# Splitting a softmax shift by batches, clearing key buffers early, and checking by a product, in a chain of four quantised transformer blocks

## The chip, the cores and the metric

The kernel runs on one core of a Trainium2 chip. The metric is the device time of one execution in microseconds (us), from the chip; lower is better. Each kernel was executed several times, and the median is quoted.

## The reference

The input x has 4 batches of 1024 tokens with 288 channels; a context of 64 tokens per batch and a mask (all zero here) come with it. Four blocks are applied one after the other, with 16 heads of 18 channels:

- Block 0: layer norm, self attention, layer norm, attention to the context, layer norm, and a feed-forward part of width 1152. All linear layers are quantised: each token's input is scaled by its largest absolute value and rounded to 8-bit levels, and the weights to levels per output channel.
- Block 1: attention to the context with two sets of keys and values ("vip"), added up.
- Block 2: self attention, context attention and a gated feed-forward part with *fake quantisation*: queries, keys, values and the probabilities of the softmax are rounded to levels of a step that belongs to the whole tensor. So the maximum over all probabilities of all batches has to be known before the first of them can be rounded.
- Block 3: as block 0, with other weights.

The cut of the reference that matters for the change is that of block 2's probabilities:

```python
def _fake_quant(x, n_bits, always_zero=False):
    levels = float(2 ** n_bits - 1)
    if always_zero:
        delta = jax.lax.stop_gradient(jnp.max(x) / levels)
        zp = jnp.float32(0.0)
```

## The kernel before

x stays in SBUF for the whole program as 32 tiles of 128 tokens (NT = 32, NTB = 8 tiles per batch). TensorE (PE) does the matmuls and the transposes, ScalarE (ACT) exponentials and copies, VectorE (DVE) reductions and rounding, GpSimd (POOL) residual additions and the affine part of the layer norms, and SyncE (SP) issues most DMAs. The framework's scheduler orders the instructions of one engine among each other; every engine then runs its own instructions strictly in that order, and a DMA queue runs in order too.

**Block 0 and block 1.** `quant_self` does the self attention of block 0. The stage after it (context attention, feed-forward, and block 1) is made of generators, such as `tokens(b, hf)` in `ctx_stage`, which do a piece of work and then yield a figure of what the next piece costs ("d8.5": 8.5 us of DVE; "a", "g" and "x" stand for other engines and waits). A planner, `run_stages`, plays these figures through and so decides in which order the pieces are emitted. The matmuls of context and vip keys (L2510, L2554), the transposes of quantised levels (L1349, copied out at L1354) and the quantised matmuls (L277) are such pieces. The statistics of a batch's layer norm come from `norm_stats`.

**Block 2, two passes.** `fq_passes` runs the self attention twice over the keys. Pass 1 (L2906, L2913) computes every score block, its exponential with the sum over keys (`sums`), and the largest exponential of each row (`top`), for 32 tiles of 16 heads: both are 128 x 512 arrays. From them `prob_shift` computes the largest probability of all, which needs a maximum over the partitions (`prob_params` calls GpSimd's partition_all_reduce, L826), and from it the step of the probabilities and, for each row, the number that has to be added to its scores so that the exponential comes out in units of that step. The shift needs a logarithm and an exponential (`log_shift`, L835 to L843; each function needs its own table in ScalarE), and it is cut into three bfloat16 parts (L2383, L2385) that add up to full precision. `watch_range` (L1218 to L1224) checks that reciprocals lie in a range.

`add_shift` (L2393 to L2400) then puts the three parts of one tile into spare channels of the queries: GpSimd copies them into a padded tile `spad`, TensorE transposes it (L2399), and VectorE adds it to the queries `qk` (L2400). The keys have ones in these channels. Pass 2 (`attend_levels`: scores L3299, exponential L3308, rounding L3311, product with the values L3282) works with key buffers `kz` in which the heads of a group are spread out; there are two, cleared once (L3006), and `spread` fills one by four DMAs (L3014). After pass 1, the order of the code is: `prob_shift` whole; loads of four parameters (L107, L113); the clearing of `spad` and `kz`; `spread(0)`; `add_shift` for the first tiles; then pass 2 with the other tiles' shifts between its score blocks.

The context attention of block 2 (`fq_tail`) calls `prob_shift` in the same way for its own probabilities. The loads of the feed-forward weights (L2408, L113), of biases (L3132) and of the first queries (L3142) follow it in SP's queue.

**The verdict.** The kernel assumes things of its data (ranges, zero points). Each assumption that is tested writes into a column of `self.bad`. At the end `verdict` takes the maximum over columns and partitions (all-reduce, L1202), reads it as an integer into the engines' registers, and a branch runs a general version of the program if it isn't zero. The last residual additions (L1747) and output DMAs (L2309) stand around it.

Of the kernel before, what the change touches and what calls it, by code (L numbers as in the profile page):

```python
# [18 lines left out]

# [2 lines left out]

# [29 lines left out]
EXP, GELU, SIDE = "exp", "gelu", "side"  # L52
# [3 lines left out]
class Net:  # L56
# [772 lines left out]

    def log_shift(self, pool, nm, sums, d, name):  # L830

        nc = self.nc
        n = sums.shape[1]
        y = pool.tile([P, n], F32, name=f"{name}y")
        nc.vector.tensor_scalar(y, sums, d, None, ALU.mult)  # L835
        z = pool.tile([P, n], F32, name=f"{name}z")
        nc.scalar.activation(z, y, AF.Ln)
        nc.vector.tensor_tensor(nm, nm, z, ALU.subtract)

        nc.scalar.activation(z, z, AF.Exp, scale=-1.0)  # L840
# [338 lines left out]
class Fast(Net):  # L1179
# [6 lines left out]
    def __init__(self, ctx, tc):  # L1186
        super().__init__(ctx, tc)
        self.bad = self.cp.tile([P, 96], F32, name="bad")
        self.n_bad = 0
        self.nmagic = self.cp.tile([P, 1], F32, name="nmagic")  # L1190
        self.nc.vector.memset(self.nmagic, -MAGIC)
        self.tiny = self.cp.tile([P, 1], F32, name="tiny")
        self.nc.vector.memset(self.tiny, 1e-8)
        self.nc.vector.memset(self.bad, 0.0)

    def verdict(self):

        nc = self.nc
        s = self.cp.tile([P, 1], F32, name="bads")
        nc.vector.tensor_reduce(s, self.bad, AX.X, ALU.max)  # L1200
        al = self.cp.tile([P, 1], F32, name="bada")
        nc.gpsimd.partition_all_reduce(al, s, P, bass_isa.ReduceOp.max)  # L1202
        fl = self.cp.tile([1, 1], mybir.dt.int32, name="badi")
        nc.vector.tensor_copy(fl, al[0:1, :])
        return nc.values_load(fl[0:1, 0:1])

    @contextmanager
# [556 lines left out]
    def quant_self(self, L, w, beside, ready):  # L1764
# [4 lines left out]
        tc, nc = self.tc, self.nc  # L1769
        with ExitStack() as es:  # L1770
# [30 lines left out]
            ep = pool(f"{L}ep", 6)  # L1801
# [5 lines left out]
            def levels(b):  # L1807

                hT = at.tile([CK, NC3, S], BF16, tag="hT", name="hT")
                srep = at.tile([P, S], F32, tag="srep", name="srep")  # L1810
                scs = []
                state[b] = {"hT": hT, "srep": srep, "sc": scs}
                stats = self.norm_stats(b, 1e-6)
# [163 lines left out]
            for b in range(B):  # L1977
                state[b]["a"] = at.tile([P, NTB, C], F32, tag="a", name="a")
                for g in range(NG):
                    if g + 1 < NG:  # L1980
                        side.insert(0, operands(b, g + 1))
                    elif b + 1 < B:
                        while side:
                            step()
                        side.append(operands(b + 1, 0))
                    if g == 1 and b + 1 < B:
                        side.append(levels(b + 1))
                        side.append(values(b + 1))
# [143 lines left out]
    def ctx_stage(self, cw, g2, b2, pool, nb):  # L2132
# [15 lines left out]
        def tokens(b, hf):  # L2148
            t0 = b * NTB + hf * 4
            if hf == 0:  # L2150
                stats[b] = self.norm_stats(b, 1e-5)
                there[b] = yield "d8.5", None, SIDE
            while b not in there:
                yield "x1", None, SIDE
            h = self.wk.tile([P, 4, C], F32, tag="h", name="h", bufs=nb)
# [209 lines left out]
    def prob_shift(self, gp, tp, top, sums, step):  # L2365


        nc = self.nc
        flat = lambda ap: ap.rearrange("p t h -> p (t h)")
        rstep = gp.tile([P, 1], F32, name="rstep")  # L2370
        nc.vector.reciprocal(rstep, step)
        r = tp.tile([P, NT * H], F32, name="rs")
        nc.vector.reciprocal(r, flat(sums))
        self.watch_range(self.R_MIN, self.R_MAX, r, "wr")
        u = flat(top)
        nc.vector.tensor_tensor(r, r, u, ALU.mult)
        pd = self.prob_params(gp, r, "pd")
        nc.vector.memset(u, 0.0)
        self.log_shift(tp, u, flat(sums), pd, "ls")
        nc.vector.tensor_scalar(u, u, rstep, None, ALU.mult)  # L2380
        parts = gp.tile([P, 3, NT * H], BF16, name="parts")
        for k in range(3):
            nc.vector.tensor_copy(parts[:, k, :], u)  # L2383
            if k < 2:
                nc.vector.tensor_tensor(u, u, parts[:, k, :], ALU.subtract)  # L2385
        return pd, parts

    def add_shift(self, qT, sp, parts, t):


        nc = self.nc
        for k in range(3):
            nc.gpsimd.tensor_copy(  # L2393
                sp[:, :, D + k : D + k + 1], parts[:, k, t * H : (t + 1) * H].unsqueeze(2)
            )
# [4 lines left out]
        nc.vector.tensor_tensor(  # L2400
            qT, qT, ps[:, : NG * P].rearrange("p (g t) -> p g t", t=P), ALU.add
        )
# [425 lines left out]
    def fq_passes(self, w, q, step, raw, rawq, qmx, qmn, side, aside):  # L2828

        tc, nc = self.tc, self.nc  # L2830
        with ExitStack() as es:
# [6 lines left out]
            v = gp.tile([P, NT, C + HP - D], BF16, name="v")  # L2838
            nc.gpsimd.memset(v[:, :, C:], 0.0)

            tops = ExitStack()
            tp = tops.enter_context(tc.tile_pool(name="f1m", bufs=1))
            top = tp.tile([P, NT, H], F32, name="top")
            sums = tp.tile([P, NT, H], F32, name="sums")
            with (
# [43 lines left out]
                for b in range(B):  # L2889
# [23 lines left out]
                                nc.vector.tensor_reduce(top[:, t, h0 : h0 + 2], e, AX.X, ALU.max)  # L2913
                    if ahead:
                        operands(b + 1, NTB - 1)
            with tops:
                pd, parts = self.prob_shift(gp, tp, top, sums, step)
            es.enter_context(self.psum("f1o"))

            pv = gp.tile([P, 1], F32, name="pv")  # L2920
            nc.vector.tensor_tensor(pv, pd, q["d"][:, 2:3], ALU.mult)
            nc.vector.tensor_scalar(wo, wo, pv, None, ALU.mult)
            at, ot, ep = pool("f1o", 1), pool("f1q", 2), pool("f1p", 2)
            g2 = self.load_bc(at, w["ln2_g"], C, "g2")
            b2 = self.load_bc(at, w["ln2_b"], C, "b2")
            bo2 = self.load_bc(at, w["bo2"], C, "bo2")
            wq2 = self.load_w(at, w["Wq2"], C, "wq2")
            spad = at.tile([P, H, HP], BF16, name="spad")
            nc.gpsimd.memset(spad, 0.0)

            def shifts(b, hf):
                for j in range(hf * 4, hf * 4 + 4):
                    t = b * NTB + j
                    self.add_shift(qk[:, b, 0, :, j * P : (j + 1) * P], spad, parts, t)
                    yield

            def output(t0, oT):

# [62 lines left out]
                        nc.sync.dma_start(rawq[t // NTB][:, t % NTB, :], y)  # L3001
                        yield

            kzs = [at.tile([P, 2, S], BF16, name=f"kz{n}") for n in range(2)]
            for kz in kzs:
                nc.gpsimd.memset(kz, 0.0)  # L3006

            def spread(n):

                kz = kzs[n % 2]  # L3010
                b, g = n // (2 * NG), n % NG
                for i in range(4):
                    rows = slice(i * HP, (i + 1) * HP)
                    nc.sync.dma_start(kz[rows, i % 2, :], qk[rows, b, 1, g, :])  # L3014

            spread(0)
            side.append(shifts(0, 0))
            while side:
                aside()
            late = []  # L3020
            for b in range(B):
                for qh in range(2):
                    side[:0] = [shifts(*divmod(2 * b + qh + 1, 2))] if 2 * b + qh + 1 < 2 * B else []
# [17 lines left out]
    def fq_tail(self, w, kq, keep, rawq, mx, nmn, beside):  # L3041
# [5 lines left out]
        with ExitStack() as es:  # L3047
# [6 lines left out]
            with (  # L3054
# [23 lines left out]
                for t in range(NT):  # L3078
# [35 lines left out]
                    e4 = self.wk.tile([P, H, T // 4], F32, tag="e4", name="e4")  # L3114
                    nc.gpsimd.tensor_tensor(e4, e2[:, :, : T // 4], e2[:, :, T // 4 :], ALU.add)
                    nc.vector.tensor_reduce(sums[:, t, :], e4, AX.X, ALU.add)
                pd, parts = self.prob_shift(gp, qp, top, sums, step)
            pv = gp.tile([P, 1], F32, name="pv")
            nc.vector.tensor_tensor(pv, pd, kq["d"][:, 1:2], ALU.mult)
            nc.vector.tensor_scalar(wo, wo, pv, None, ALU.mult)  # L3120
# [121 lines left out]
                before = t0  # L3242
            for _ in spare:
                pass
            self.weave([forward(before)], 1, 1)

    def scale_register(self, name, t):
# [176 lines left out]
```

## Time and profile before

| | |
|---|---|
| median of 3 runs | 5156.69 us (5151.0 to 5164.89) |
| the profiled execution | 5151.01 us, span 5149.3 us, mean granted TensorE clock 0.837 |
| busy share of the span | PE 85%, PE weight loads 34%, DVE 57%, ACT 61%, POOL 27% |
| instructions | 63938 |
| block 0 self attention | 0 to about 890 us |
| block 0 context, feed-forward, block 1 | 890 to 1664 us |
| block 2: layer norm, projections | 1664 to 1850 us |
| pass 1; gap; pass 2 | 1850 to 2437; to 2467; to 3023 us |
| queries, context pass, second gap | 3023 to 3200 us |
| probabilities and feed-forward | 3200 to 3846 us |
| block 3 | 3846 to 5149 us |

A profile is one execution with a record of each instruction: its engine, line, operands, start and duration. "Idle before" is the time in which the engine had nothing running before the instruction, followed by what ended it; "issue" means that no recorded event explains it. Lines are those of the kernel before, unless the kernel after is meant.

### The profile page before, as it was taken

The numbers are of one execution on the slowest core, as the hardware profiler recorded it, in microseconds if no ns is written. First come the engines' busy times: TensorE is split into PE (matmuls) and PEld (weight loads), VectorE is DVE, ScalarE is ACT, GpSimd is POOL, SyncE is SP. The second block draws the span as 40 slices with busy tenths as digits, with TensorE's granted clock in tenths as the row PEclk, the third lists the DMA queues.
The fourth block names the chain that finished last, engine by engine and source line by source line (L and its number), as shares of the span: only waits on it lengthen the run. The fifth ranks groups of instructions, "written<-read, shape, count | busy, mean of one in ns | idle before, by whom it ended". The sixth has DMA issues, their size and how long they took to land. (4 is left out here: it accounts for less than half of the span.)

```text
span 5149.3 us, 63938 instructions
## 1 busy us (share of the span) xinstructions
PE 4374.8 (85%) x23291; PEld 1746.7 (34%) x23291; DVE 2952.4 (57%) x6478; ACT 3130.4 (61%) x4422; POOL 1394.7 (27%) x2173
## 2 busy tenths in 40 slices
PE   5999998788898979998688864899988999996786
PEld 2223222445566421100233332454542223222343
DVE  8333244665554579999688777332334334334775
ACT  3766666466653259998888853222215666674796
POOL 4020111542321566200222234111113111103664
PEclk8999998889999965555788775899997999997897
DMA  2000001200001221000000032000000000001000
GB/s 75 4 5 12 3 21 46 75 27 14 3 12 38 110 84 38 11 1 0 23 26 24 24 98 77 21 15 10 1 15 1 8 4 9 18 21 31 16 17 20
DMA packets 135639, 136.01 MB, mean 26 GB/s; under 512 B 69260, under 2 KB 111884, under 8 KB 133648
## 3 DMA queue, kind: packets, MB, share of 16 engines
q1 hardware_dynamic: 134112, 128.13, 8.3%
q0 software_dynamic: 1200, 3.69, 0.3%
q8 instruction: 185, 3.03, 0.2%
q14 instruction: 142, 1.16, 0.1%
HBM read 79.92 MB, written 43.47 MB: 24 GB/s over the span
## 5 line engine op out<-in xcount | busy, mean ns | idle before, releaser
L2004 ACT ACTIVATE e<-ps 128x1024 f32<-128x1024 f32 x1024 | 998.6, 1021 | 483.1 <-PE ps L1994 473.0
L1994 PE MATMUL ps<-qT,kT 32*128 32x512 f32 x4096 | 704.1, 662 | 4.4 <-ACT e L2004 4.4
L1954 PE MATMUL ps<-e,v 128*32 128x512 f32 x4096 | 575.7, 627 | 10.2 <-DVE oT L1965 7.7
L2913 DVE TENSOR_REDUCE top<-e 128x2 f32<-128x2048 f32 x256 | 561.9, 2275 | 18.5 <-ACT e L2906 18.5
L2906 ACT ACTIVATE e<-ps 128x1024 f32<-128x1024 f32 x512 | 534.1, 1369 | 19.6 <-PE ps L3259 11.3
L3308 ACT ACTIVATE e<-ps 128x1024 f32<-128x1024 f32 x512 | 483.9, 1059 | 88.0 <-PE ps L3299 70.5
L3259 PE MATMUL ps<-qk 32*128 32x512 bf16 x1024 | 511.1, 604 | 24.3 <-ACT e L2906 23.0
L1747 POOL TENSOR_TENSOR x<-x,y 128x288 f32<-128x288 f32 x192 | 151.9, 802 | 826.4 <-DVE y L1746 759.1
L1404 POOL TENSOR_TENSOR h<-h,g 128x288 f32<-128x288 f32 x224 | 181.5, 813 | 645.0 <-ACT h L1401 606.1
L3311 DVE TENSOR_SCALAR eb<-e 128x2048 bf16<-128x2048 f32 x256 | 322.1, 1261 | 49.1 <-ACT e L3308 46.7
L1994 PEld LDWEIGHTS ps<-qT,kT 32*128 32x128 f32 x4096 | 205.4, 189 | 228.8 <-issue 146.2
L2906 ACT ACTIVATION_READ_ACCUMULATOR e<-ps 128x1 f32 x512 | 280.8, 550 | 0.0
L3299 PE MATMUL ps<-qk,kz 64*128 64x512 bf16 x1024 | 225.0, 436 | 47.8 <-ACT e L3308 45.3
L2437 PE MATMUL psf<-hT,w 128*128 128x512 f32 x576 | 257.9, 600 | 0.6 <-ACT hT L2429 0.6
L1954 PEld LDWEIGHTS ps<-e,v 128*32 128x32 f32 x4096 | 83.2, 109 | 422.8 <-issue 349.4
L1349 PE MATMUL ps<-idb,q 128*128 128x128 bf16 (+2 forms) x1152 | 112.8, 242 | 122.4 <-ACT q L1333 68.5
L1401 ACT ACTIVATE h<-x,nmr,rstd 128x288 f32<-128x288 f32 x224 | 130.2, 622 | 140.1 <-DVE nmr L1393 69.1
L3208 ACT ACTIVATE gl<-psf,bf 128x512 f32<-128x512 f32 x72 | 46.0, 684 | 270.8 <-PE psf L2441 266.2
L3259 PEld LDWEIGHTS <-qk 32*128 32x128 bf16 x1024 | 52.9, 99 | 464.9 <-issue 464.9
L1354 ACT COPY qT<-ps 98x384 bf16<-98x384 bf16 (+3 forms) x256 | 151.6, 641 | 71.2 <-PE ps L1349 71.0
L1405 POOL TENSOR_TENSOR h<-h,b 128x288 f32<-128x288 f32 x224 | 180.0, 807 | 0.3
L277 PEld LDWEIGHTS <-qT 98*128 98x128 bf16 (+2 forms) x1344 | 135.1, 104 | 128.8 <-issue 45.8
(483 smaller groups left out, 7672.3 us busy)
## 6 DMA issues: line engine op xcount, KB each, us to landing
raw<-y SPq DMA_DIRECT2D x32, 432.0 KB
in<-raw SPq DMA_DIRECT2D x32, 432.0 KB
kz<-qk SPq DMA_DIRECT2D x128, 64.0 KB
wn<-in_L_wfc SPq DMA_DIRECT2D x12, 432.0 KB
x<-in_x SPq DMA_DIRECT2D x4, 1152.0 KB
vvo<-vt SPq DMA_DIRECT2D x16, 288.0 KB
vo<-vvo SPq DMA_DIRECT2D x4, 1152.0 KB
rawq<-y SPq DMA_DIRECT2D x32, 144.0 KB
```

Of the source, the lines that this page charges most:

```text
L1404: nc.gpsimd.tensor_tensor(h, h, g, ALU.mult)
L1405: nc.gpsimd.tensor_tensor(h, h, beta, ALU.add)
L1954: nc.tensor.matmul(acc[i * HP : (i + 1) * HP, :], lhsT=st["v"][:, kt, h * (D + 1) : h * (D + 1) + HP], rhs=es_[i // 2][:, i % 2, :], start ...
L1994: nc.tensor.matmul(pss[i // 2][:, i % 2, :], lhsT=self.row_tile(kT, i)[:, kt * P : (kt + 1) * P], rhs=self.row_tile(qT, i)[:, qh * 512 : ( ...
L2004: nc.scalar.activation(e, ps, AF.Exp, scale=SCALE)
L2437: nc.tensor.matmul(o, lhsT=lhs(i)[:, c, :], rhs=rhs(i)[:, c, :], start=(c == 0), stop=False)
L2906: nc.scalar.activation(e[:, j, :].rearrange("p (a n) -> p a n", a=2), sc, AF.Exp, scale=rstep, accum_out=sums[:, t, h0 + j : h0 + j + 1],)
L2913: nc.vector.tensor_reduce(top[:, t, h0 : h0 + 2], e, AX.X, ALU.max)
L3259: self.nc.tensor.matmul(ps[:, c, :], lhsT=self.row_tile(qT, i)[:, g, qt * P : (qt + 1) * P], rhs=self.row_tile(kT, i)[:, g, c * 512 : (c + ...
L3299: nc.tensor.matmul(pss[i][:, n, :], lhsT=kz[rows, i, kt * P : (kt + 1) * P], rhs=qT[rows, g, qh * 512 : (qh + 1) * 512], start=True, stop= ...
L3308: nc.scalar.activation(e[:, 2 * n : 2 * n + 2, :], ps, AF.Exp, scale=step)
L3311: nc.vector.tensor_scalar(eb, e, MAGIC, MAGIC, ALU.add, ALU.subtract)
```

## The change

- `verdict` sums the flags over the partitions by a matmul with a column of ones, in a PSUM pool of its own, instead of the all-reduce.
- `prob_shift` no longer computes the whole shift. It returns two functions: `shift[0]` for the tiles of batch 0 (128 columns), `shift[1]` for the other three batches (384 columns). The parts lie in two tiles, from which `add_shift` picks. The two share one pair of scratch buffers. The watch of the range comes behind them. In the context pass of block 2 both functions are called one after the other.
- In `fq_passes` the key buffers are allocated and cleared ahead of pass 1, and `spread(0)` is emitted right after pass 1's code, ahead of `prob_shift`; the first pad too. The first four tiles' shifts come between `shift[0]` and `shift[1]`; the loads, and a second pad for the other tiles, come after. The pool of pass 1's exponentials keeps its four buffers.
- The statistics of batch 0 for block 0's context stage and for the self attention of block 3 are emitted earlier, and the planner's figure for that piece is "d0" instead of "d8.5".

```diff
     def verdict(self):
...
-        al = self.cp.tile([P, 1], F32, name="bada")
-        nc.gpsimd.partition_all_reduce(al, s, P, bass_isa.ReduceOp.max)
         fl = self.cp.tile([1, 1], mybir.dt.int32, name="badi")
-        nc.vector.tensor_copy(fl, al[0:1, :])
+        with self.psum8("bad"):
+            ps = self.ps1()
+            nc.tensor.matmul(ps[0:1, 0:1], lhsT=s, rhs=self.ones[:, 0:1], start=True, stop=True)
+            nc.vector.tensor_copy(fl, ps[0:1, 0:1])
...
+                    if (b, g) == (B - 1, 2):
+                        self.early["ctx"] = self.norm_stats(0, 1e-5)
...
-                stats[b] = self.norm_stats(b, 1e-5)
-                there[b] = yield "d8.5", None, SIDE
+                stats[b] = self.norm_stats(b, 1e-5) if b else self.early.pop("ctx")
+                there[b] = yield "d8.5" if b else "d0", None, SIDE
...
     def prob_shift(self, gp, tp, top, sums, step):
...
-        self.watch_range(self.R_MIN, self.R_MAX, r, "wr")
-        u = flat(top)
-        nc.vector.tensor_tensor(r, r, u, ALU.mult)
-        pd = self.prob_params(gp, r, "pd")
-        nc.vector.memset(u, 0.0)
-        self.log_shift(tp, u, flat(sums), pd, "ls")
...
+        nc.vector.tensor_tensor(flat(top), r, flat(top), ALU.mult)
+        pd = self.prob_params(gp, flat(top), "pd")
+        parts = [gp.tile([P, 3, n * H], BF16, name=f"parts{n}") for n in (NTB, NT - NTB)]
+        yz = [tp.tile([P, (NT - NTB) * H], F32, name=f"ls{n}") for n in "yz"]
+
+        def shift(n):
+            tiles = slice(NTB, NT) if n else slice(0, NTB)
+            u = flat(top[:, tiles, :])
+            nc.vector.memset(u, 0.0)
+            self.log_shift_in(u, flat(sums[:, tiles, :]), pd, *(t[:, : u.shape[1]] for t in yz))
+            nc.vector.tensor_scalar(u, u, rstep, None, ALU.mult)
+            for k in range(3):
+                nc.vector.tensor_copy(parts[n][:, k, :], u)
+                if k < 2:
+                    nc.vector.tensor_tensor(u, u, parts[n][:, k, :], ALU.subtract)
+            if n:
+                self.watch_range(self.R_MIN, self.R_MAX, r, "wr")
+
+        return pd, parts, [partial(shift, n) for n in range(2)]
...
+            at = pool("f1o", 1)
+            kzs = [at.tile([P, 2, S], BF16, name=f"kz{n}") for n in range(2)]
+            for kz in kzs:
+                nc.gpsimd.memset(kz, 0.0)
...
-            with tops:
-                pd, parts = self.prob_shift(gp, tp, top, sums, step)
+            spread(0)
+            spad = tp.tile([P, H, HP], BF16, name="spad")
+            nc.gpsimd.memset(spad, 0.0)
+            pd, parts, shift = self.prob_shift(gp, tp, top, sums, step)
             es.enter_context(self.psum("f1o"))
...
+            shift[0]()
+            for _ in shifts(0, 0, spad):
+                pass
+            shift[1]()
+            tops.close()
...
-            spad = at.tile([P, H, HP], BF16, name="spad")
+            spad = at.tile([P, H, HP], BF16, name="spad2")
...
-                pd, parts = self.prob_shift(gp, qp, top, sums, step)
+                pd, parts, shift = self.prob_shift(gp, qp, top, sums, step)
+                for f in shift:
+                    f()
...
+            self.early["self"] = self.norm_stats(0, 1e-6)
             self.weave([forward(before)], 1, 1)
```

More of the change, by code (lines that the diff above doesn't have):

```diff
@@ L21 @@
 from contextlib import ExitStack, contextmanager
+from functools import partial
 import concourse.bass as bass
@@ L830, in log_shift, with log_shift_in @@
     def log_shift(self, pool, nm, sums, d, name):
+        n = sums.shape[1]
+        self.log_shift_in(nm, sums, d, *(pool.tile([P, n], F32, name=f"{name}{k}") for k in "yz"))
+    def log_shift_in(self, nm, sums, d, y, z):
         nc = self.nc
-        n = sums.shape[1]
-        y = pool.tile([P, n], F32, name=f"{name}y")
         nc.vector.tensor_scalar(y, sums, d, None, ALU.mult)
-        z = pool.tile([P, n], F32, name=f"{name}z")
         nc.scalar.activation(z, y, AF.Ln)
@@ L1189, in __init__ @@
         self.n_bad = 0
+        self.early = {}
         self.nmagic = self.cp.tile([P, 1], F32, name="nmagic")
@@ L1812, in levels @@
                 state[b] = {"hT": hT, "srep": srep, "sc": scs}
-                stats = self.norm_stats(b, 1e-6)
+                stats = self.early.pop("self", None) if b == 0 else None
+                if stats is None:
+                    stats = self.norm_stats(b, 1e-6)
                 yield
@@ L2373, in prob_shift @@
         nc.vector.reciprocal(r, flat(sums))
-        self.watch_range(self.R_MIN, self.R_MAX, r, "wr")
-        u = flat(top)
-        nc.vector.tensor_tensor(r, r, u, ALU.mult)
-        pd = self.prob_params(gp, r, "pd")
-        nc.vector.memset(u, 0.0)
-        self.log_shift(tp, u, flat(sums), pd, "ls")
[L2380 to L2386, printed above, removed]
+        nc.vector.tensor_tensor(flat(top), r, flat(top), ALU.mult)
[15 more added lines that the diff above has]
+        return pd, parts, [partial(shift, n) for n in range(2)]
     def add_shift(self, qT, sp, parts, t):
         nc = self.nc
+        u = t - NTB if t >= NTB else t
         for k in range(3):
             nc.gpsimd.tensor_copy(
-                sp[:, :, D + k : D + k + 1], parts[:, k, t * H : (t + 1) * H].unsqueeze(2)
+                sp[:, :, D + k : D + k + 1],
+                parts[t >= NTB][:, k, u * H : (u + 1) * H].unsqueeze(2),
             )
@@ L2839, in fq_passes, with spread @@
             nc.gpsimd.memset(v[:, :, C:], 0.0)
+            at = pool("f1o", 1)
+            kzs = [at.tile([P, 2, S], BF16, name=f"kz{n}") for n in range(2)]
+            for kz in kzs:
+                nc.gpsimd.memset(kz, 0.0)
+            def spread(n):
+                kz = kzs[n % 2]
+                b, g = n // (2 * NG), n % NG
+                for i in range(4):
+                    rows = slice(i * HP, (i + 1) * HP)
+                    nc.sync.dma_start(kz[rows, i % 2, :], qk[rows, b, 1, g, :])
             tops = ExitStack()
@@ L2915, in fq_passes, with shifts @@
                         operands(b + 1, NTB - 1)
-            with tops:
-                pd, parts = self.prob_shift(gp, tp, top, sums, step)
+            spread(0)
+            spad = tp.tile([P, H, HP], BF16, name="spad")
+            nc.gpsimd.memset(spad, 0.0)
+            pd, parts, shift = self.prob_shift(gp, tp, top, sums, step)
             es.enter_context(self.psum("f1o"))
+            def shifts(b, hf, spad):
+                for j in range(hf * 4, hf * 4 + 4):
+                    t = b * NTB + j
+                    self.add_shift(qk[:, b, 0, :, j * P : (j + 1) * P], spad, parts, t)
+                    yield
+            shift[0]()
[3 more added lines that the diff above has]
+            tops.close()
             pv = gp.tile([P, 1], F32, name="pv")
@@ L2922, in fq_passes @@
             nc.vector.tensor_scalar(wo, wo, pv, None, ALU.mult)
-            at, ot, ep = pool("f1o", 1), pool("f1q", 2), pool("f1p", 2)
+            at, ot, ep = pool("f1s", 1), pool("f1q", 2), pool("f1p", 2)
             g2 = self.load_bc(at, w["ln2_g"], C, "g2")
@@ L2927, in fq_passes @@
             wq2 = self.load_w(at, w["Wq2"], C, "wq2")
-            spad = at.tile([P, H, HP], BF16, name="spad")
+            spad = at.tile([P, H, HP], BF16, name="spad2")
             nc.gpsimd.memset(spad, 0.0)
[L2931 to L2935, printed above, removed]
             def output(t0, oT):
@@ L3002, in queries @@
                         yield
[L3004 to L3019, printed above, removed]
             late = []
@@ L3022, in fq_passes @@
                 for qh in range(2):
-                    side[:0] = [shifts(*divmod(2 * b + qh + 1, 2))] if 2 * b + qh + 1 < 2 * B else []
+                    side[:0] = [shifts(*divmod(2 * b + qh + 1, 2), spad)] if 2 * b + qh + 1 < 2 * B else []
                     oT = ot.tile([P, NG, 512], F32, tag="oT", name="oT")
```

## The prediction

> **What bounds the kernel now.** The page's busy shares (TensorE 85%, ScalarE 61%) average over stages with different limits, so I went by stages: busy time in windows, then the timeline around the places that the change touches, then the waits. Four places are touched: the gap between the two passes of block 2 (2432 to 2468 us), the gap before block 2's own context pass (3164 to 3200), the end (5128 to 5149), and the stage after block 0's self attention (890 to 1664), whose order a planner makes anew.
>
> First the timeline of the first gap (start, duration, engine, line, operation; in brackets the idle time before it and what ended it):
>
> ```profile
> 2432.99 1.28 ACT L837 ACT_TABLE_LOAD   x1
> ...
> 2444.92 0.69 DVE L824 TENSOR_REDUCE pds<-rs 128x1 f32<-128x512 f32 x1
> ...
> 2446.87 0.63 ACT L837 ACTIVATE lsz<-lsy 128x512 f32<-128x512 f32 x1 [12.60 <-DVE lsy L835]
> ...
> 2447.51 1.28 ACT L840 ACT_TABLE_LOAD   x1
> ...
> 2454.28 0.43 DVE L2383 CAST parts<-top 128x512 bf16<-128x512 f32 x1
> ...
> 2455.31 0.74 POOL L107 DMA_DIRECT2D g<-in_L_ln_g  x1 [9.19 <-DVE parts L2383]
> ...
> 2457.58 3.56 POOL L3006 MEMSET kz<- 128x2048 bf16 x2
> ...
> 2461.08 0.52 POOL L2393 COPY spad<-parts 128x16 bf16<-128x16 bf16 x3
> ...
> 2467.49 1.46 PE L3299 MATMUL ps<-qk,kz 64*128 64x512 bf16 x6
> ...
> 2468.14 4.69 ACT L3308 ACTIVATE e<-ps 128x1024 f32<-128x1024 f32 x5 [18.70 <-PE ps L3299]
> ```
>
> The last maximum of pass 1 ends near 2439.4; until 2467.5 TensorE has no attention work. It is one chain: vector arithmetic over all 512 columns until 2454.71, GpSimd's queue (three loads, two kinds of memset) until 2461.08, then five tiles of copies and transposes. Pass 2 after it is ScalarE's: in the window 2467 to 3023 line L3308 is busy 483.9 us of 556. An earlier first exponential therefore moves the whole pass, and what follows, by as much.
>
> The second gap, same view:
>
> ```profile
> 3179.14 0.49 DVE L2383 CAST parts<-top 128x512 bf16<-128x512 f32 x1
> 3179.78 0.39 SPq L2408 DMA_DIRECT2D w<-in_L_Wff  x1
> ...
> 3180.74 10.31 SPq L3132 DMA_DIRECT2D bf<-in_L_bff  x1
> ...
> 3191.23 1.77 SPq L3142 DMA_DIRECT2D qT<-qb  x2
> ...
> 3199.09 1.52 DVE L2400 TENSOR_TENSOR qT<-qT,ps 128x512 bf16<-128x512 bf16 x4 [19.46 <-DMA qT<-qb]
> ```
>
> Here the first queries (qT) wait in SP's queue behind the weights and the 10.31 us bias issue, and that queue starts when the last cast frees its pool. A later last cast is paid one for one.
>
> The end:
>
> ```profile
> 5132.97 0.52 DVE L1746 SCALAR_TENSOR_TENSOR y<-ps,sc,wfc2sw 128x288 f32<-128x288 f32 x1 [2.48 <-PE ps L277]
> 5134.13 0.38 POOL L1202 PARTITION_ALL_REDUCE bada<-bads  x1 [5.80 <-DVE y L1746]
> ...
> 5141.97 1.53 POOL L1747 TENSOR_TENSOR x<-x,y 128x288 f32<-128x288 f32 x2 [7.46 <-issue]
> ```
>
> The last two tiles are added on GpSimd at 5141.97, though their inputs were there at 5130.49 and 5133.49. In between stands the all-reduce of the verdict, with 5.80 us of nothing before and 7.46 us after.
>
> **The change part by part.** The profiled execution is 5151.01 us with a span of 5149.3; it is the lowest of the three runs, 5.7 us under their median 5156.69. Terms are worked out in the trace; the sum is set on the median.
>
> *First gap, arithmetic.* The range watch moves behind the product, so the two reduces in front (0.69 and 0.68, overlapping) go: pds ends at 2444.71 instead of 2445.61, 0.9 earlier, and the logarithm starts 0.9 earlier too. Only 128 columns go first. A 512-column ACTIVATE takes 0.63 and a 128x256 copy 0.35 to 0.37, so I take 0.25 for 128 columns: Ln at 2445.8 to 2446.05, the table load of 1.28 to 2447.35, Exp to 2447.62. The nine vector steps then took 5.24 us (2449.47 to 2454.71); at 128 columns I take 0.28 for a two-input one (0.69 for 512 columns, 0.46 for 288), 0.27 and 0.21 for the others, 2.4 in all. But the instruction order puts two or three steps of the other 384 columns (about 0.55 each) between them, which wait for a second Ln. So the third part is done near 2452.05 instead of 2454.71: **-2.7**. If the 384 columns never got in the way it would be -4; if all their steps up to their own addition did, -1.5.
>
> *First gap, GpSimd.* In the new order the copies follow the all-reduce at once; loads and the clearing of a second pad come behind the first four tiles, the key buffers are cleared at the start of block 2. From the cast's end to the first copy it was 6.37 us; 0.05 is left: **-6.3**. A library switch before a copy is not shown: after the other all-reduce (3170.52 to 3170.90) a copy runs at 3177.18, right after its cast. Were there one of 7.46 us as at the end, the copies could start at 2452.7, 0.6 later than I take. *Fifth tile.* TensorE transposed a fifth tile (2466.95) ahead of the first score; in the new order the first score follows the fourth tile's addition: **-0.8**. First matmul 2457.6 instead of 2467.5. The rest of the shift and the loads then run beside five exponentials of 0.94 us each; tile five's copies come near 2461.8, when ScalarE still has work until 2462.8. So I give back 0, at most 1. **First gap -9.8 (-7 to -11).**
>
> *What was moved earlier.* The two key memsets (3.56) and the pad's (0.54) now stand on GpSimd ahead of the load of g1 in block 2. GpSimd idles 44.98 us there until 1653.99, and the memsets wait only for block 0's last residual add (1608.23): 0; without that cover the first h*g at 1660.74 is up to 4.1 later. The eight key DMAs (5.88 of SP's queue) stand among the raw loads of pass 1, after the twelfth; the early keys are copied by then, and those loads wait for GpSimd's buffers anyway (55.2 us in 7 waits): 0, up to +2 if one of them came to be late. Their pools keep the four buffers of pass 1.
>
> *Second gap.* Both shifts run in full here, nothing is overlapped. There are two more table loads (2 x 1.28 = 2.56), and the 384-column logarithm shares its buffer with the 128-column exponential; twelve more vector instructions are filled with work of the other columns. The watch behind gives 0.9 back. Last cast about 3181.0 instead of 3179.63: **+1.3 (0.5 to 2.5)**. The Trainium skill (ScalarE: Activation LUTs, section What ACT_TABLE_LOAD costs) charges each switch about 2.66 us, the load of 1283 ns and a drain of 1380 ns. The trace agrees on the load (1.28) and shows no drain: Ln ends at 2447.50, the load starts at 2447.51 and Exp at 2448.81. By the page this term would be some 2.8 us larger, and the change, which has four more switches, that much worse.
>
> *The verdict.* Without the all-reduce the adds run when their inputs are there: 5130.6 and 5133.6 to 5134.35 instead of 5143.50. The flag's one-column matmul and copy stand where TensorE and VectorE have ended, beside the output DMA; the read of the flag in SP (5143.9) followed the last output issue already. What follows the last add stays 5.8 us. **-9.2 (-7 to -10).** The Trainium skill (GPSIMD Engine Reference, section Engine selection) gives a reduce along partitions to GpSimd, which speaks against this part, and its section Instruction dispatch puts the first call of a freshly loaded kernel at about 6 us. The trace has 5.80 in front of a 0.38 us all-reduce, near that figure, and 7.46 behind it, which the page does not name; by the page's figure alone the part would be worth 6.
>
> *Early statistics.* The instruction order ahead of block 0's context stage is the same on every engine: the scheduler had moved those statistics up already. At the start of block 3 only VectorE's order shifts a little: 0 (-0.5 to +0.5). What does change is the planner's figure for batch 0, from 8.5 us of VectorE to 0, and from it the order of all engines between 890 and 1664. TensorE is busy 652.66 of those 774 us, so 121 is all that any order could win. The old plan held batch 0 8.5 us later than the trace does; I take half of that, **-4**, between +8 and -10.
>
> Sum: -9.8 + 1.3 - 9.2 - 4 = -21.7, so 5129.3 on the profiled execution and **5135** on the median.
>
> **The rivals.** *The new order of block 0's stage loses.* TensorE runs in order, and in the new one in the instruction order it changes line 638 times between the last self-attention score of block 0 and block 2, against 597. What a change can cost is seen in the waits of that window (us in total, times, longest):
>
> ```profile
> ACT qT L1354 <- PE ps L1349: 52.3, 27, 8.4
> ...
> PEld L277 <- issue: 25.7, 52, 5.5
> ```
>
> A wait of a copy for a transpose is 1.94 us on average (52.3 in 27), a weight load's issue 0.49. The 41 changes cost between 41 x 0.49 = 20 and 41 x 1.94 = 80 if each pays; half at the higher price is +40. With the other terms at -17.7 that is 5179, slower. The point is a loss of over 33 us. Against it: most of these groups are pieces of the context keys' preparation put between ready work.
>
> *The first gap gives less.* Ln, Exp, Ln, Exp could keep the 384 columns in front, and TensorE, in order, could stand at tile five's transposes until ScalarE runs dry: +4 of the -9.8, 5139. For it: the order puts steps of the 384 columns before the last 128-column cast. Against: those transposes stand behind ten score matmuls, enough for five exponentials.
>
> *The new order wins.* If the opening (TensorE busy 32 of the 60 us from 890) fills, the stage may give 12 to 20 us: 5119 to 5127.
>
> *The end does not shorten*, if something else holds the adds: 5144. The 7.46 us row with "issue" is the only doubt; I fold it into the forecast's spread.
>
> **How the numbers follow.** About 0.3% (15.5 us) is what can be told from no change. Forecast 0.62 (0.56 faster, 0.06 within the bound); re-planned order loses 0.20 (half within the bound, half slower); first gap gives less 0.08 (half faster, half the same); re-planned order wins 0.10, faster. Faster 0.70, same 0.20, slower 0.10. The range runs from the better half of the winning order, 5116, to a stage loss of about 24 us, 5163; beyond lie the rest of the loss (about 0.13) and of the gain (0.05).
>
> **What would show it.** Right: first pass-2 exponential about 26 us after the start of the last of pass 1 rather than 36; the first GpSimd copy within 0.1 us of a cast; qT about 1.3 us later after the second reciprocal; the last add at once after the last y, and the end 5.8 us later. Wrong: a GpSimd idle of 6 to 7 us between all-reduce and copies; a wait of ScalarE on TensorE in the first 10 us of pass 2; or the time from the last self-attention score to block 2's first LayerNorm different by more than 10 us, which would outweigh the rest.

## The result and the profile after

The kernel after takes 5133.05 us (median of 5 runs, 5125.84 to 5133.78) against 5156.69; the ratio is 0.9953, 95% interval 0.9941 to 0.9964, so 19 to 30 us faster. The forecast was 5135. The sum came out, but most of its large terms did not: it is a story of errors that cancel.

I cut the profiled executions into stretches between instructions that both kernels have. "Stage" runs from the first of the last residual terms of block 0's self attention (VectorE's y, 879.69 before) to block 2's first h*g on GpSimd (1660.74); each later stretch begins where the one above it ends.

| stretch, us | before | after | difference |
|---|---|---|---|
| to the end of block 0's self attention | 879.7 | 880.2 | +0.5 |
| stage: block 0's context and feed-forward, block 1 | 781.05 | 772.7 | -8.4 |
| to pass 1's first exponential | 204.4 | 203.5 | -0.9 |
| pass 1, to its last exponential | 566.8 | 566.8 | +0.1 |
| first gap, to pass 2's first exponential | 36.3 | 27.05 | -9.2 |
| 32 exponentials on | 29.3 | 33.6 | +4.3 |
| to the 512th, and to the second reciprocal | 666.7 | 665.6 | -1.1 |
| second gap, to the first addition to qT | 34.95 | 36.7 | +1.8 |
| to the last y of block 3 | 1933.9 | 1932.3 | -1.5 |
| to the end | 16.3 | 9.2 | -7.1 |

The timeline of the first gap, kernel after (start, duration, engine, line, operation; idle before):

```profile
2436.19 0.38 POOL L827 PARTITION_ALL_REDUCE pdd<-pds  x1 [338.18 <-DVE pds L825]
...
2437.11 0.31 ACT L840 ACTIVATE lsz<-lsy 128x128 f32<-128x128 f32 x1 [11.49 <-DVE lsy L839]
...
2443.22 0.22 DVE L2397 CAST parts<-top 128x128 bf16<-128x128 f32 x1
...
2443.50 0.32 POOL L2411 COPY spad<-parts 128x16 bf16<-128x16 bf16 x1 [1.13 <-DVE parts L2397]
...
2450.27 4.76 ACT L3337 ACTIVATE e<-ps 128x1024 f32<-128x1024 f32 x5 [7.56 <-PE ps L3328]
...
2451.33 0.74 POOL L108 DMA_DIRECT2D g<-in_L_ln_g  x1 [2.98 <-ACT e L3337]
...
2454.01 0.54 POOL L2976 MEMSET spad<- 128x512 bf16 x1
2454.62 0.52 POOL L2411 COPY spad<-parts 128x16 bf16<-128x16 bf16 x3
...
2456.39 1.02 ACT L3337 ACTIVATE e<-ps 128x1024 f32<-128x1024 f32 x1 [1.36 <-PE ps L3328]
...
2459.32 13.16 ACT L3337 ACTIVATE e<-ps 128x1024 f32<-128x1024 f32 x14 [1.90 <-PE ps L3328]
```

No library switch stands between the all-reduce and the copies (the trace's next record of one, MODIFY_POOL_CONFIG, is at 2523.6), and the third copy starts 0.06 us after the third cast. Five exponentials run, and then ScalarE stops twice: 1.36 us because the fifth tile's copies stand on GpSimd behind three loads and a memset, and 1.90 us behind the sixth tile's copies, which start 1.33 us after the fifth's and take 1.58 us instead of 0.52.

The second gap and the end, same view and kernel:

```profile
3165.63 0.36 DVE L2397 CAST parts<-top 128x384 bf16<-128x384 f32 x1
3166.14 0.38 SPq L2427 DMA_DIRECT2D w<-in_L_Wff  x1
...
3186.11 1.52 DVE L2419 TENSOR_TENSOR qT<-qT,ps 128x512 bf16<-128x512 bf16 x4 [20.13 <-DMA qT<-qb]
```

```profile
5118.44 0.52 DVE L1751 SCALAR_TENSOR_TENSOR y<-ps,sc,wfc2sw 128x288 f32<-128x288 f32 x1 [2.64 <-PE ps L278]
...
5119.04 0.79 POOL L1752 TENSOR_TENSOR x<-x,y 128x288 f32<-128x288 f32 x1 [2.37 <-DVE y L1751]
5119.31 0.14 DVE L1209 CAST badi<-ps 1x1 int32<-1x1 f32 x1 [0.35 <-PE ps L1208]
```

The last addition starts 0.6 us after its input does; before, the two last additions started 9.0 us after the last input did (5132.97 to 5141.97). But the span ends at 5127.7, 7.8 us after that addition; before it was 5.8.

### The profile page after: what moved, and what is told of

It reads as the page before. It is cut to its first block, busy times and chain, and to the rows that moved or that the text cites. A ratio compares the mean times of both kernels' runs of the same rounds, so it can differ in the third digit from the quotient of the medians.

```text
span 5127.7 us, 63962 instructions
## 1 busy us (share of the span) xinstructions
PE 4382.1 (85%) x23293; PEld 1744.4 (34%) x23293; DVE 2965.3 (58%) x6502; ACT 3136.1 (61%) x4430; POOL 1400.5 (27%) x2173
## 5 line engine op out<-in xcount | busy, mean ns | idle before, releaser
L1359 ACT COPY qT<-ps 128x640 bf16<-128x640 bf16 (+3 forms) x256 | 153.0, 641 | 78.1 <-PE ps L1354 77.8
```

## The experiments

Each was timed against the kernel before on the same chip, except the last three, which are single executions with a profile. Stretches are those of the table.

**1. The planner's figure alone.**

```diff
-                there[b] = yield "d8.5", None, SIDE
+                there[b] = yield ("d8.5" if b else "d0"), None, SIDE
```

> The kernel before with nothing but the planner's figure for batch 0 changed from d8.5 to d0; in block 0's stage every engine then has the order of the kernel after. Theory: the order is what the stage gains. From the last pair of residual terms of the self attention (VectorE's two y at 879.69 before, 880.23 after) to GpSimd's load of g for block 2 it was 774.3 us before and 766.5 after; here about 766.5, and the whole kernel 8 us under before, near 5149. Rival: the 7.9 us are scatter between two executions; then 774 here, and no difference in the whole.

Measured: 5143.34 us, ratio 0.9975 (0.9963 to 0.9988); stage 769.9. (The expectations of 1 and 2 count only to GpSimd's load of g, 6 to 7 us earlier: 763.7 here, 774.3 before.) One number given to the planner is worth about half of the whole change. Busy time and clock over this stretch, kernel before and then this one (duration, then busy time of PE, weight loads, DVE, ACT, POOL, each with its count, the clock, the DMA share and rate):

```profile
879.70:1660.75 781.05, 655.83 (x4027) 415.92 (x4026) 445.02 (x1354) 437.57 (x736) 271.05 (x488) 0.90 0.10 31
```

```profile
886.50:1656.36 769.86, 661.86 (x4023) 413.25 (x4023) 451.91 (x1353) 435.62 (x736) 270.74 (x488) 0.90 0.10 31
```

TensorE idles 781.05 - 655.83 = 125.2 us before and 108.0 now; 17.2 us less, of which 6.0 are given back in longer busy time.

**2. The kernel after with the old figure.**

```diff
-                there[b] = yield "d8.5" if b else "d0", None, SIDE
+                there[b] = yield "d8.5", None, SIDE
```

> The kernel after with the figure d8.5 put back; the early statistics stay, and block 0's stage has the order of before on every engine. Theory: about 774 us for that stretch, everything else as after, so 8 us over after: near 5141. Rival (scatter, or the early statistics themselves bring it): 766 and 5133.

Measured: 5149.87 us, ratio 0.9988 (0.9979 to 0.9997). The early statistics bring the stage nothing by themselves. It takes 787.4, 781.3 to the load of g and not 774, and not even the 781.05 of before in the same order: 6 us that neither theory had.

**3. The verdict alone.**

```diff
-        nc.gpsimd.partition_all_reduce(al, s, P, bass_isa.ReduceOp.max)
...
+            nc.tensor.matmul(ps[0:1, 0:1], lhsT=s, rhs=self.ones[:, 0:1], start=True, stop=True)
```

> The kernel before with nothing but the verdict by a matmul. Theory: from the start of the last y to the end 9.3 us instead of 16.3, because the branch on the flag (about 3.5 us on GpSimd) no longer runs beside the wait for the library but after the last addition; -7.1 us, near 5149.6. Rival (the forecast): what follows the last addition stays 5.8 us, so 7.2 us from the last y to the end, -9.2. Second rival: the end is as late as before because something else holds the additions: 0.

Measured: 5153.45 us, ratio 0.9994 (0.9986 to 1.0003). From the last y to the end it is 9.06 us, close to the theory's 9.3; these -7.3 us are at the edge of the timed interval (-7.2 to +1.5 us), and the whole alone would not have shown them.

**4. Block 2's part alone**, without the verdict's, the statistics' and the planner's edits.

> The kernel before with the split shift, the early key buffers and the two pads, in both passes; without the verdict's change, the early statistics and the planner's figure. Theory: first exponential of pass 2 starts 27.0 us after the last of pass 1 (36.3 before), then ScalarE waits about 3.3 us around the fifth tile's transposes, and from the second reciprocal to the first addition to qT it is 36.7 instead of 35.0: -9.2 + 3.2 + 1.8 = -4.2, near 5152.5. Rival: pass 2 of the kernel after was 3 us longer by scatter; then the gap stays whole, -7.4, near 5149.

Measured: 5159.11 us, ratio 1.0006 (0.9995 to 1.0017). The largest part of the change, for which the forecast had -8.5, gives nothing or costs a little. Gap 27.05, next 32 exponentials 33.55 (4.2 more than before, 3.2 expected), second gap 36.2; and again a longer stage, 786.3. The timelines around the clearing of the key buffers show why. Kernel before:

```profile
1609.05 0.77 DVE L143 TENSOR_SCALAR h<-x,mv,rstd 128x288 f32<-128x288 f32 x2 [0.90 <-POOL x L1747]
1609.73 2.47 DVE L2642 TENSOR_TENSOR ev<-ev,ps 128x512 f32<-128x512 f32 x4
...
1610.56 0.41 PE L2417 MATMUL ps<-idf,x 128*128 128x128 f32 x2 [1.96 <-DVE ev L2642]
...
1612.65 3.72 PE L2437 MATMUL ps<-xT,wq 128*128 128x256 f32 x16 [0.60 <-ACT xT L2429]
```

This kernel:

```profile
1612.34 3.90 DVE L144 TENSOR_SCALAR h<-x,mv,rstd 128x288 f32<-128x288 f32 x2 [0.90 <-POOL x L1750]
1612.36 3.71 POOL L2857 MEMSET kz<- 128x2048 bf16 x2
1616.02 0.68 POOL L2945 MEMSET spad<- 128x512 bf16 x1
1616.15 2.46 DVE L2655 TENSOR_TENSOR ev<-ev,ps 128x512 f32<-128x512 f32 x4
...
1616.97 0.66 PE L2430 MATMUL ps<-idf,x 128*128 128x128 f32 x2 [5.08 <-DVE ev L2655]
...
1620.02 6.19 PE L2450 MATMUL ps<-xT,wq 128*128 128x256 f32 x16 [0.60 <-ACT xT L2442]
```

GpSimd had nothing else to do; but VectorE's two normalisations, 0.77 us, take 3.90: each ends 0.16 to 0.17 us after one of GpSimd's memsets, which take 3.71. Behind them in VectorE's order stand the products for which TensorE waits: 5.08 us instead of 1.96. All six kernels that clear on GpSimd (after, 2, 4, 5, 6, 11) show a wait of 5.1 to 5.3 us there, and the five that do not clear early (before, 1, 3, 9, 10) one of 1.96 or 1.97.

After that wait TensorE is slower too: sixteen matmuls take 6.19 us instead of 3.72. This goes with TensorE's granted clock, 0.66 in the 15 us from the normalisations' start on, where the kernel before had 1.00; but the clearing is not needed for it. Experiment 9, without the clearing and with the short wait, has the slow matmuls too, at a clock of 0.77 (experiment 3 likewise, 6.36 us at 0.77):

```profile
1599.94 0.41 PE L2417 MATMUL ps<-idf,x 128*128 128x128 f32 x2 [1.96 <-DVE ev L2642]
...
1602.21 6.52 PE L2437 MATMUL ps<-xT,wq 128*128 128x256 f32 x16 [0.58 <-ACT xT L2429]
```

So the 3.1 us of longer wait are the clearing's, and of the 2.5 us behind it that is not shown.

**5. The fifth tile.** On top of the kernel after, the second pad stands beside the key buffers, VectorE clears it early, SP issues the three loads instead of GpSimd, and the range watch stands ahead of the shifts:

```diff
+            spad2 = at.tile([P, H, HP], BF16, name="spad2")
...
+            nc.vector.memset(spad2, 0.0)
...
-            g2 = self.load_bc(at, w["ln2_g"], C, "g2")
...
+                nc.sync.dma_start(d, w[k].partition_broadcast(P))
```

> The kernel after with the second pad allocated beside the key buffers and cleared early by VectorE, and the three parameter loads issued by SP, so that between the fourth and the fifth tile's copies GpSimd has nothing else; the range watch stands before the shift again, since its array is reused as scratch. Theory: the 4.1 us that pass 2 loses in its first 33 exponentials (29.4 before, 33.5 after) are those loads and that memset in front of the fifth tile; they go: gap 27.1 and 29.4 again, -4 against after, near 5129. Rival: it is the slower copies (1.58 us for three beside VectorE's rounding, 0.52 alone); then 33 exponentials still take 32 to 33 us and the whole is as after.

Measured: 5130.18 us, ratio 0.9954 (0.9939 to 0.9969). Gap 27.2, and the next 32 exponentials take 29.8 again: 3.8 us are back. ScalarE now runs twenty exponentials in one piece where it ran five:

```profile
2451.44 18.44 ACT L3337 ACTIVATE e<-ps 128x1024 f32<-128x1024 f32 x20 [7.56 <-PE ps L3328]
```

By the medians the whole shows 3 of them, by the ratios (0.9954 against 0.9953) none; either is within its scatter.

**6. One shift for all columns.**

```diff
-        parts = [gp.tile([P, 3, n * H], BF16, name=f"parts{n}") for n in (NTB, NT - NTB)]
+        parts = [gp.tile([P, 3, NT * H], BF16, name="parts")]
...
-            shift[1]()
```

> The kernel after with one shift over all 512 columns (two table loads, nine vector steps) in both passes; everything else stays, the clearing and the order of the copies before the loads too. Theory by my steps: the split is worth 1.5 to 2 us in the gap (28.7 instead of 27.05), and about as much comes back at the fifth tile, whose loads in front start at the same time; the second gap is 1.6 shorter (35.1 instead of 36.7). So -1.5 against after, not to be seen in the whole. Rival: the split carries the gap's gain; then the gap is 31 or more and the whole 3 us slower than after.

Measured: gap 28.7, next 32 exponentials 32.7, second gap 35.3; 5141.68 us, ratio 0.9974 (0.9963 to 0.9984). So the split carries 1.6 of the gap's 9.2 us; the other 7.6 are the order on GpSimd, the watch behind the product and the missing fifth tile. The local numbers say -0.7 against the kernel after, the whole says +8.6. The profile has longer stretches where nothing was edited (2.6 us in pass 2, 2.7 before the second reciprocal, 2.4 up to block 3). What lengthens them stays open. Of the 8.6 us of the whole a part goes with the granted clock: its mean is 0.837 over the nine executions and 0.840 over the five of the kernel after, and among the 35 executions of the kernel before timed beside experiments 1 to 4, 0.001 less goes with 2.1 us more.

**7. The clearing on VectorE.** On top of the kernel after, `nc.vector.memset` for the key buffers and the first pad.

> The kernel after with the early clearing of key buffers and first pad on VectorE instead of GpSimd. Theory: beside GpSimd's memset of 3.71 us VectorE's two TENSOR_SCALAR over 128x288 take 3.90 us instead of 0.77, TensorE waits 5.1 instead of 2.0 for VectorE and then runs slower for some 15 us; so the stretch from the self attention's last residual terms to the first h*g of block 2 is 2.8 to 5 us longer than without the clearing (772.7 against 769.9; 786.3 to 787.4 against 781.1 to 782.5). On VectorE the clearing costs about 1 us each and the two keep 0.77: near 770, -2.5 against after. Rival: those stretches differ by scatter or by where the instructions lie; then 772.7 as after.

Measured: 5125.22 us, ratio 0.9941 (0.9926 to 0.9957); stage 767.8. VectorE, this kernel:

```profile
1597.16 0.77 DVE L144 TENSOR_SCALAR h<-x,mv,rstd 128x288 f32<-128x288 f32 x2 [0.90 <-POOL x L1752]
1598.09 0.91 DVE L2863 MEMSET kz<- 128x1024 uint32 x1 [0.16 <-issue]
```

The 0.77 is back, and each clearing costs 0.91 us: what slowed VectorE was the memset on GpSimd. TensorE's wait is 2.99 us. Of the 4.9 us by which the stage is shorter, part is scatter, as experiment 8 will show (771.2 with the same clearing).

**8. Both, with a whole shift in the second gap.**

> e5 and e7 together, with the split kept in the first gap and one whole shift in the second. Sum of their parts against after: -4 (fifth tile) -2.5 (clearing on VectorE) -1.6 (second gap) = -8, near 5125. Rival: the first exponential being early makes pass 2 wait elsewhere, and -4 of it is lost: near 5129.

Measured: 5123.99 us (5122.3 to 5125.9), ratio 0.9939 (0.9925 to 0.9953): the fastest of all, under both kernels by the median, though its interval overlaps that of the kernel after. First gap 27.2, next 32 exponentials 29.8, second gap 35.1.

**9 and 10. Other figures for the planner**, on the kernel before: "d4" and "d7".

> The kernel before with the planner's figure for batch 0 at d4, half of the old one; the planner gives an order that is neither that of before nor that of after. Theory: the figure is wrong by what the statistics have long been done, and the stage gains as the figure approaches 0; so the stretch from the self attention's last residual terms to block 2's first h*g lies between 770 (d0) and 782 (d8.5), near 776. Rival: the order's worth has nothing to do with how true the figure is, any change of it draws another order; then it lies anywhere from 765 to 800, outside 770 to 782 as likely as inside.

> As e9_plan_d4 with d7, again a new order. Theory: close to before, 779 to 782. Rival: anywhere from 765 to 800.

Measured: stage 772.0 and 768.6, the whole 5138.98 and 5155.18 in one execution each. (In that of 10 other stretches are longer than before, 4.1 us up to the second reciprocal and 4.4 up to the last y, so its whole hardly shows the stage.) Both theories fall. The gain doesn't follow the figure, and it isn't a new draw each time. TensorE's matmuls in the stage (busy, mean ns | idle before them, and what ended it), kernel before:

```profile
L277 PE MATMUL ps<-wfc1T,qT 98*128 98x384 bf16 x288 | 56.0, 339 | 15.4 <-ACT qT L1354 9.1 <-DVE a L2232 4.8 <-DVE tops L2281 1.1
L277 PE MATMUL ps<-wfc2T,qT 128*128 128x288 bf16 x288 | 41.0, 291 | 5.5 <-ACT qT L1354 5.3 <-ACT ec L2204 0.3
L2201 PE MATMUL ps<-qcT,kbd 64*128 64x512 f32 x128 | 43.0, 641 | 5.3 <-ACT ec L2204 3.7 <-DVE tops L2281 0.8 <-ACT qT L1354 0.8
L2212 PE MATMUL ps<-ec,vbd 128*64 128x512 f32 x128 | 37.6, 659 | 8.0 <-DVE a L2232 4.8 <-DVE y L1746 2.5 <-ACT ec L2204 0.7
L1349 PE MATMUL ps<-idb,q 128*128 128x128 bf16 (+2 forms) x576 | 52.8, 236 | 31.8 <-ACT q L1333 18.5 <-POOL q L1611 7.2 <-DVE y L1746 4.9
```

Figure 0 (experiment 1):

```profile
L277 PE MATMUL ps<-wfc1T,qT 98*128 98x384 bf16 x288 | 61.5, 363 | 3.7 <-ACT qT L1354 3.3 <-ACT ec L2204 0.4
L277 PE MATMUL ps<-wfc2T,qT 128*128 128x288 bf16 x288 | 42.6, 296 | 0.6 <-ACT qT L1354 0.6
L2201 PE MATMUL ps<-qcT,kbd 64*128 64x512 f32 x128 | 44.5, 656 | 0.8 <-ACT ec L2204 0.8
L2212 PE MATMUL ps<-ec,vbd 128*64 128x512 f32 x128 | 37.4, 632 | 0.7 <-ACT ec L2204 0.7
L1349 PE MATMUL ps<-idb,q 128*128 128x128 bf16 (+2 forms) x576 | 55.0, 233 | 41.4 <-ACT q L1333 27.6 <-POOL q L1611 9.1 <-DVE y L1746 3.4
```

In front of the feed-forward's quantised matmuls (L277) and the context attention's (L2201, L2212) the idle time falls from 34.2 to 5.8 us; in front of the transposes of levels (L1349) it grows from 31.8 to 41.4. Figure 7 has the same pattern (6.1 and 39.1). The orders at 0, 4 and 7 differ only in the first 70 us of the stage; the planner falls into one arrangement for each of the three, and into another at 8.5. Why its search tips between 7 and 8.5 was not looked into.

**11. The end without the branch.** The kernel after without the read of the flag, the branch and the general version; the flag itself is computed.

> The kernel after without the read of the flag, the branch and the general version behind it; the flag is still computed. Theory: the 2.0 us by which the end after the last y was later than forecast (9.2 instead of 7.2) are the branch on GpSimd, which in the kernel before ran beside the wait for the library; then 7.2 us or less here. Rival: it is the output's own way out, with two of its DMAs issued later than before; then 9 us remain.

Measured: 4.47 us from the last y to the end, instead of 8.8 to 9.2 in the seven kernels that have the matmul and the branch. The read, the branch and the general version behind it cost 4.3 to 4.8 us. The trace's records of the branch fit: on GpSimd it begins at 5120.0 in the kernel after, half a microsecond after the flag, and the engine goes on at 5123.6; in the kernel before it began at 5135.3, while the additions still waited until 5142 for the library, whose switch the trace records at 5134.5.

**The stage cut in two.** The order and the clearing act in different parts of the stage. Cut where the two normalisations start (1609.05 before, 1612.34 in experiment 4, 1597.16 in experiment 7), the traces of all runs separate them:

| order; clearing | runs | to the normalisations, us | from there to the first h*g, us |
|---|---|---|---|
| old; late | before, 3 | 729.4, 729.5 | 51.7, 52.9 |
| old; early on GpSimd | 2, 4 | 731.1, 729.5 | 56.3, 56.8 |
| new; late | 1, 9, 10 | 718.6, 719.1, 717.1 | 51.2, 53.0, 51.5 |
| new; early on GpSimd | after, 5, 6, 11 | 716.9, 715.9, 714.7, 715.0 | 55.8, 56.7, 56.4, 55.8 |
| new; early on VectorE | 7, 8 | 715.0, 717.4 | 52.8, 53.7 |

On average the new order is 13 us shorter up to the cut, and no run of one order lies among those of the other. Behind the cut the clearing on GpSimd costs 4.2 us in the old order and 4.3 in the new, again without overlap; on VectorE it costs some 1.3, little more than the runs differ. (The granted clock makes part of the differences: of the late ones, the three at 51.2 to 51.7 had 1.00 in the 15 us behind the cut, the two at 52.9 and 53.0 had 0.77.)

## Why the prediction was right, and where its steps were not

- *First gap, arithmetic and GpSimd's queue:* right. Counted from the last exponential of pass 1, the third part came 2.6 us earlier (2.7 forecast), and 0.06 us lie between cast and copy instead of 6.4.
- *First gap, fifth tile:* the 0.8 did not come: the four tiles took 5.74 us from first transpose to first score, as five did (5.83), since copies lengthened to 0.90 beside VectorE's steps. And "I give back 0, at most 1" failed. I had the copies at 2461.8, a microsecond before ScalarE ran dry. The loads and the memset in front of them began when the other columns' shift freed its memory and took 3.3 us, so the copies started only 0.4 us before ScalarE ran dry; the next two tiles' copies then took 1.58 instead of 0.52 beside the rounding. Measured +4.3: the rival "the first gap gives less" had this mechanism and this price, at a chance of 0.08.
- *What was moved earlier:* "0" failed. I asked only whether GpSimd was idle, not whom its memset slows. Behind the cut it costs some 4 us, in the new order as in the old, 3.1 of them TensorE's longer wait (5.1 against 2.0); in the whole stage the scatter of the rest nearly hides it. The Trainium skill (GPSIMD Engine Reference, section Specifications) says that GpSimd shares its SBUF interfaces with VectorE and that there is contention with VectorE's instructions in a 2-port perf mode or with two SBUF inputs. The trace agrees that the two engines hold each other up, 3.90 against 0.77; in which mode the normalisations run, no row says. This page would have spoken against the edit.
- *Second gap:* right, +1.1 to +1.8 in six profiles against +1.3; the last 384-column cast was the gate, as the steps had it.
- *Verdict:* the additions moved as forecast, but "what follows the last add stays 5.8 us" failed, it is 7.4 to 7.8: the branch lay hidden beside the library's return and came out; -7.1 instead of -9.2 (-7.1 to -7.6 in seven profiles).
- *Early statistics:* 0 was right (2). *The new order:* -4 was mis-sized, and its range of +8 to -10 missed. Measured -13 up to the cut, and -13 as the whole of experiment 1. My reason, half of 8.5, had nothing to do with it: the figures 4 and 7 give about the same (9, 10). The price I set on more changes of line on TensorE was no price: with more of them it idles less. The rival "the new order wins" had the size, 12 to 20 us, but not the place: the opening does not fill, TensorE is busy 32.4 of the 60 us from 890 in both kernels.

Set against each other: -8.5 was forecast for block 2's part, and it gave nothing (4); -13.2 for the rest, and it gave -13 for the order and some -7 for the end. The errors are of about one size and of opposite sign, so that the whole came out at 5133 for 5135 by luck; the first gap's arithmetic and the second gap were foreseen.

## What to carry to other kernels

Idle time of an engine doesn't make its work free: ask whose instructions it lengthens, and look at durations of the neighbour's instructions, not only at waits. When a step is taken out of a queue, follow the queue to the next thing that a late consumer needs (here the fifth tile) and to whatever had been hidden beside the step (here the branch). And when a planner's input is touched, its new order is a change in its own right: run it alone first. Where two effects sit in one stage, cut the stage between them: the whole stage showed 8 us, the two parts -13 and +4.

## What the runs showed of the hardware

- A GpSimd memset of 128 x 2048 bfloat16 (1.9 us each) holds up a VectorE TENSOR_SCALAR of 128 x 288 float32 until it ends: 3.90 us for two beside 3.71 us of memset, 0.77 alone. The other way round, GpSimd's three copies of 128 x 16 take 1.58 us beside VectorE's rounding (1.23), 0.52 alone.
- The same sixteen matmuls (128x256, float32) take 3.72 us where the granted clock was 1.00 over the 15 us around them (before, 1, 10) and 5.4 to 6.5 us where it was 0.66 to 0.89 (all other runs). A long wait in front is not needed for it: 6.36 and 6.52 after waits of 1.97 and 1.96 (3, 9).
- Reading a flag and branching on it, with the general version behind, cost 4.3 to 4.8 us at the end of the program (11). A GpSimd all-reduce costs 0.38 us and about 13 around it when the same engine's ordinary operations stand before and behind it at the end (5.80 and 7.46), and nothing that shows when the engine has long been idle before it and copies follow (first gap).
- Executions of nearly the same instructions differ by up to 7 us by the end of block 0's self attention (879.4 to 886.4), which is why single stretches tell more here than the whole.
